# Attention maxima turned by VectorE and written as rows, values taken from the keys' projection, two sequences' mixed weights per step

## The chip, the cores and the metric

The kernel runs on one core of one Trainium2 chip. The time is the device time of one execution in microseconds (us); of several executions the median is given.

## What is computed

Four sequences of 512 tokens, 256 features. A gated network chosen per sequence gives `c`; attention with 16 heads of 16 features, all heads sharing one key and one value, works on `c`; then an expert layer. The change concerns the attention:

```
q = (c @ Wq.T + bq) * 16**-0.5          # 16 heads x 16
k, v = split(c @ Wkv.T + bkv)           # 16 each, shared by the heads
w = softmax(q_rows @ k.T)               # q_rows: 16*512 rows per sequence
x = x + (w @ v, heads side by side) @ Wo.T + bo
x2 = cond2(x, cond_8)                   # weights mixed per sequence from 8 sets
x = x + moe(x2)                         # router, top 2 of 8 experts, gelu
```

All of it is in float32.

## The kernel before

Work is issued in an order written out by hand; each engine (TensorE, VectorE, ScalarE, GpSimd) and SyncE, which issues most DMAs, takes its own instructions strictly in that order and waits on semaphores.

*Layout.* `q` of a sequence is a tile of 128 partitions x 4 x 512. Partition 32j + d, for j from 0 to 3 and d below 16, holds feature d; rows 32j+16 to 32j+31 are zero. `k` has the same four groups of 32 rows (the same keys four times), with ones in rows 32j+16 to 32j+31. So a matmul over 32 rows gives q.k, and a number put into row 32j+16 (`HD` is 16) of the query side is added to the scores. Four such matmuls, on the four groups of 32 rows, run on TensorE side by side.

*Units and steps.* A unit `u` is a quarter of the rows of a sequence (`b, hg = divmod(u, 4)`), 16 in all; a step is a quarter of a unit, 64 in all. The loop at L1049 goes over `n`. In step n it issues

- `maxima(m)` (L379) for m = n + 6: four matmuls L388 into PSUM banks, of which tag "m" has three and tag "x" four, and four VectorE reductions L392 to negated row maxima in `negm`;
- `exponentials(n)` (L412): four matmuls L420 of keys with shifted queries `qs`, and ScalarE's exponential L421;
- `weigh(n - 1)` (L426): eight matmuls L435 that weigh the values with the exponentials; after the fourth step of a unit a copy L444 and a DMA L445 to DRAM (`od`);
- the side work of the step, from the lists `beside` and `last` (L724 to L759): projections of the next sequence, and normalising, output projection, routing of the former ones.

A matmul of float32 is two records in the profile, a transpose one. A *pass* below is two maxima and two exponentials, in four row groups at once. In a *dense* step (side work on TensorE, L1071) the order is pass, side work, pass, all of `weigh`; in an *open* step (L1083) it is pass, half of `weigh`, pass, side work, other half.

*The shift.* `shifted(u)` (L396), at steps with m % 4 == 1, turns `negm` with four TensorE transposes L402 into one bank, so that the maxima lie in rows 32j+16, and VectorE adds that bank to the unit's columns of `q` (L406). The sum `qs` is what `exponentials` reads.

*Side work touched.* `queries` (L316) projects half of the queries, ScalarE brings them to `stage`, and SyncE copies them in eight DMAs L327 into `q`; `q` alternates between two tiles. `keys` L333 and `values` L340: the values are eight matmuls L345 of 32 columns with the tokens as stationary operand, then VectorE adds the bias L349. The values tile has 32 columns, those from 16 on are one, so the same matmul gives the softmax sum. In the steps of sequence b (k = n % 16): queries of b+1 at k = 0 and 1, keys at 2, values at 3. `values` of `finish` (L451), at k = 2, is of another kind: it loads sums (L456) and weighed values (L460) of sequence b-1 back from `od`; `inverse` (L482), at k = 3, takes their reciprocal on VectorE (L485), writes it (L486) and reads it back spread out (L490). Sequence 0 has its projections before the loop, where `hidden` and `down` (the gated network) fill TensorE.

*Mixed weights.* While sequence 0 is in the loop, `turn_mixed` (L690: four transposes L695 and a ScalarE copy) and `route_mixed` (L701: matmuls L707 with the router) prepare one sequence each: steps 5, 7, 9, 11 turn, steps 6, 8, 10, 12 route (`behind`, L762).

After the loop the expert layer streams its weights; TensorE is busy there throughout.

Of the kernel before, what the change touches and what calls it, by code (L numbers as in the profile page):

```python
# [17 lines left out]
P = 128  # L18
B = 4
# [22 lines left out]
def adaln_attn_ffn_kernel(  # L42
# [9 lines left out]
    bk: bass.AP,  # L52
    wv: bass.AP,
    bv: bass.AP,
    wo: bass.AP,
# [132 lines left out]
    bk_sb = load(bk, [P, 1], "bk_sb")  # L188
    wv_sb = load(wv, [P, 2, 32], "wv_sb")
    bv_sb = load(bv[0:1, :].to_broadcast([P, 32]), [P, 32], "bv_sb")  # L190
    wo_sb = load(wo, [P, 2, D], "wo_sb")
# [48 lines left out]
    for n in range(2):  # L240
        t = const.tile([P, 4, 4, 32], F32, name=f"negm{n}")
        nc.gpsimd.memset(t, 0.0)
        negm.append(t)

    q_tiles = []
    for n in range(2):
        t = const.tile([P, 4, T], F32, name=f"q{n}")
        nc.gpsimd.memset(t, 0.0)
        q_tiles.append(t)

    def mixed(b, g):
# [47 lines left out]
    seqs = [{} for _ in range(B)]  # L299
    qs_of = {}  # L300
    e_of = {}
# [9 lines left out]
    def project(b):  # L311
# [4 lines left out]
        def queries(co):  # L316
            def piece():
                pq = bank("x")
                for c in range(2):
                    mm(pq, wq_sb[:, c, ts(co, P)], coT[:, c, ts(b, T)], start=c == 0, stop=c == 1)  # L320
                qd = qp.tile([P, T], F32, name="stage", bufs=4)
                nc.scalar.activation(
                    qd, pq, AF.Identity, bias=bqs_sb[:, co : co + 1], scale=HD**-0.5
                )
                for n in range(2):
                    for j in range(4):
                        nc.sync.dma_start(  # L327
                            s["q"][32 * j : 32 * j + HD, 2 * co + n, :],
                            qd[ds(64 * n + HD * j, HD), :],
                        )  # L330
            return piece

        def keys():  # L333
            s["k"] = qp.tile([P, T], F32, name="k")
            pk = bank("x")
# [4 lines left out]
        def values():  # L340
            s["v"] = qp.tile([P, 4, 32], F32, name="v")
            pv = bank("x")
            for sc in range(4):
                for c in range(2):
                    mm(  # L345
                        pv[:, ts(sc, 32)], coT[:, c, ds(b * T + sc * P, P)], wv_sb[:, c, :],
                        start=c == 0, stop=c == 1,
                    )
            nc.vector.tensor_tensor(  # L349
                s["v"], pv[:, 0:P].rearrange("p (s d) -> p s d", s=4),  # L350
                bv_sb.unsqueeze(1).to_broadcast([P, 4, 32]), ALU.add,
            )
# [26 lines left out]
    def maxima(m, js):  # L379
# [6 lines left out]
        for j in js:  # L386
# [5 lines left out]
            nc.vector.tensor_reduce(  # L392
                nm[:, i, j, HD : HD + 1], pm, AX.X, ALU.max, negate=True
            )

    def shifted(u):  # L396

        b, hg = divmod(u, 4)
        nm = negm[u % 2]
        pt = bank("x")  # L400
        for i in range(4):
            nc.tensor.transpose(  # L402
                pt[:, ts(i, P)], nm[:, i].rearrange("p j d -> p (j d)"), ident
            )
        qs = qp.tile([P, 512], F32, name="qs")
        nc.vector.tensor_tensor(  # L406
            qs.rearrange("p (i t) -> p i t", i=4), pt.rearrange("p (i t) -> p i t", i=4),
            seqs[b]["q"][:, :, ts(hg, P)], ALU.add,
        )
        qs_of[u] = qs  # L410

    def exponentials(n, js):  # L412
# [4 lines left out]
        for n4, j in enumerate(js):  # L417
            px = bank("m" if n4 >= 2 else "x")
            rows_j = slice(32 * j, 32 * j + 32)
            mm(px, k[rows_j, ts(sc, P)], qs_of[u][rows_j, :], start=True, stop=True)  # L420
            nc.scalar.activation(  # L421
# [339 lines left out]

    behind = {5 + 2 * b + n: (f, b) for b in range(B) for n, f in enumerate((turn_mixed, route_mixed))}  # L762

# [10 lines left out]
    def side(b, k):  # L774
# [14 lines left out]
        if b == 0 and k in behind:  # L789
            f, to = behind[k]  # L790
            f(to)


# [8 lines left out]
    for m in range(LEAD):  # L802
        maxima(m, (0, 1, 2, 3))
        if m == 5:
            shifted(0)
# [243 lines left out]
    for n in range(STEPS + 1):  # L1049
# [7 lines left out]
        )  # L1057
        turning = m <= STEPS + 1 and m % 4 == 1
        if m >= STEPS:
            if n < STEPS:  # L1060
                exponentials(n, (0, 1, 2, 3))
            if turning:
                shifted(m // 4 - 1)
            if n == STEPS:
# [6 lines left out]
        elif dense:  # L1071

            maxima(m, (0, 1))
            exponentials(n, (2, 3))
            if turning:
                shifted(m // 4 - 1)
            side(b, k)
# [5 lines left out]
        else:  # L1083
# [6 lines left out]
            exponentials(n, (0, 1))  # L1090
            if turning:
                shifted(m // 4 - 1)
            side(b, k)
            if n > 0:
                weigh(n - 1, (0, 1))

    places = itertools.count()
# [73 lines left out]
def _layouts(i):  # L1171
# [8 lines left out]
    def quarters(w):  # L1180
# [14 lines left out]
    wk = np.zeros((P, 2, 4, 32), f32)  # L1195
    wk[..., :HD] = wkv[:, :, None, :HD]
    bk = np.ones((4, 32), f32)
    bk[:, :HD] = bkv[:HD]
    wv = np.zeros((P, 2, 32), f32)
    wv[..., :HD] = wkv[..., HD:]  # L1200
    bv = np.ones((1, 32), f32)
    bv[0, :HD] = bkv[HD:]
    bias2 = i["L0_cond2_bias"]
# [12 lines left out]
        "bk": bk.reshape(P, 1),  # L1216
        "wv": wv,
        "bv": bv,
        "wo": halves(i["L0_attn_Wo"].T),
# [33 lines left out]
```

## Time and profile before

| | |
|---|---|
| median of 3 runs | 688.33 us (687.2 to 688.59) |
| profiled execution | 676.98 us |
| its span, first to last instruction | 675.3 us |
| granted TensorE clock | 0.994 |
| attention steps, in the span | about 107 to 394 us |

| stretch of the span (us) | TensorE busy | VectorE busy | ScalarE busy |
|---|---|---|---|
| 0 to 75 (gated network) | 72.53 | 30.44 | 14.54 |
| 75 to 107 (its end, first maxima) | 32.00 | 20.70 | 4.81 |
| 107 to 394 (attention steps) | 284.14 | 203.06 | 157.99 |
| 394 to 675 (expert layer) | 267.77 | 75.43 | 48.47 |

| group | line | count | mean ns of one |
|---|---|---|---|
| maxima, matmul records | L388 | 500 | 639 |
| exponentials, matmul records | L420 | 512 | 639 |
| weighing, matmul records | L435 | 1024 | 387 |
| reduction to maxima | L392 | 256 | 685 |
| transposes of the maxima | L402 | 64 | 286 |
| adding them to q | L406 | 16 | 682 |
| values, matmul records | L345 | 64 | 271 |
| their bias | L349 | 4 | 290 |

In profile lines PE is TensorE, DVE VectorE, ACT ScalarE, POOL GpSimd, SP SyncE; "SPq" is what its queue issues. A timeline line has start and duration in us, engine, line, operation, output and inputs, and a count of merged instructions. Matmuls are pipelined, so their durations overlap; distances between starts tell what a group takes.

### The profile page before, as it was taken

To read this page: it belongs to the slowest core of one execution; us is meant where nothing else is said; L and a number is where in the kernel's file an instruction comes from. 1 tells how busy PE (TensorE), PEld (TensorE's weight loads), DVE (VectorE), ACT (ScalarE), POOL (GpSimd) and SP (SyncE) were. 2 spreads that over 40 slices of the span, in tenths; PEclk is the share of its full clock that TensorE was granted. 3 is DMA by queue.
4 is the path that set the end of the run, shared out by engine and by line. 5 is a ranking of instruction groups with operands and counts; after the bars stand their busy time and mean duration, and the time that the engine had idled before them with its cause. 6 is when DMAs were issued, how large, how long until landed. Compare 5 with 4: busy or idle time off the path is not lost.

```text
span 675.3 us, 10833 instructions
## 1 busy us (share of the span) xinstructions
PE 656.4 (97%) x4106; PEld 406.9 (60%) x4106; DVE 329.6 (49%) x782; ACT 225.8 (33%) x400; POOL 118.0 (17%) x149
## 2 busy tenths in 40 slices
PE   8999999999999999999999999999999999999992
PEld 3444433444344433443335368888999999988881
DVE  1174855666667677766897754264222222221110
ACT  1122114555554555455553651222111111121110
POOL 1710000000000000310013041135332222232331
PEclk9999999999999999999999999999999999999997
DMA  6931992100031101330024199537989999975311
GB/s 215 376 108 28 248 259 66 33 17 17 11 96 56 48 17 54 116 103 17 21 85 166 64 323 336 161 106 232 277 255 329 330 323 317 337 235 153 82 22 26
DMA packets 63483, 102.40 MB, mean 152 GB/s; under 512 B 6464, under 2 KB 26560, under 8 KB 63296
## 3 DMA queue, kind: packets, MB, share of 16 engines
q1 hardware_dynamic: 47536, 81.51, 35.7%
q0 software_dynamic: 7008, 10.56, 7.6%
q10 hardware_dynamic: 8880, 9.57, 5.5%
q8 instruction: 34, 0.56, 0.3%
q14 instruction: 25, 0.20, 0.1%
HBM read 75.37 MB, written 24.15 MB: 147 GB/s over the span
## 4 chain that ended last, share of the span: by engine, by line
PE 92%; DVE 3%; DMA 2%; issue 1%; POOL 0%; ACT 0%; SPq 0%; POOLq 0%; DVEq 0%
PE ps_m L983 19%; PE ps_m L388 19%; PE ps_x L1013 17%; PE ps_a L435 9%; PE ps_a L286 4%; PE ps_x L270 4%; PE ps_x L288 4%; PE ps_x L420 3%; PE ps_x L547 2%; PE ps_x L320 2%; PE ps_x L515 2%; PE ps_x L402 1%; DVE negm L392 1%; PE ps_x L337 1%; PE ps_a L968 1%; PE ps_x L345 1%
## 5 line engine op out<-in xcount | busy, mean ns | idle before, releaser
L392 DVE TENSOR_REDUCE negm<-ps_m 128x1 f32<-128x512 f32 x250 | 160.6, 685 | 73.3 <-PE ps_x L420 60.1
L421 ACT ACTIVATE e<-ps_x 128x512 f32<-128x512 f32 x244 | 132.4, 594 | 119.8 <-PE ps_x L420 115.9
L388 PE MATMUL ps_m<-k,q 32*128 32x512 f32 x500 | 150.4, 639 | 0.1
L420 PE MATMUL ps_x<-qs,k 32*128 32x512 f32 x488 | 139.9, 639 | 0.0
L983 PE MATMUL ps_m<-xT,wi_sb 128*128 128x128 f32 (+1 forms) x800 | 130.3, 321 | 0.0
L1013 PE MATMUL ps_x<-wo_sb,e 128*128 128x256 f32 x576 | 128.5, 379 | 0.0
L983 PEld LDWEIGHTS ps_m<-xT,wi_sb 128*128 128x128 f32 x800 | 119.0, 191 | 10.1 <-issue 0.4
L1013 PEld LDWEIGHTS ps_x<-wo_sb,e 128*128 128x128 f32 x576 | 107.6, 190 | 13.7
L987 ACT ACTIVATE e<-ps_m 128x512 f32<-128x512 f32 x72 | 42.8, 597 | 194.1 <-PE ps_m L983 192.6
L1024 POOL DMA_INDIRECT out_dram<-y,to_row x36 | 56.1, 1558 | 140.5 <-DMA out_dram<-y,to_row 74.4
L388 PEld LDWEIGHTS ps_m<-k,q 32*128 32x128 f32 x500 | 44.6, 183 | 54.3 <-issue 23.9
L435 PE MATMUL ps_a<-e,v 128*32 128x256 f32 x1024 | 73.7, 387 | 1.4 <-ACT stage L444 1.0
L435 PEld LDWEIGHTS ps_a<-e,v 128*32 128x32 f32 x1024 | 24.2, 108 | 70.6 <-issue 54.4
L970 DVE COPY xT<-ps_a 128x256 f32<-128x256 f32 (+1 forms) x23 | 12.2, 529 | 95.1 <-PE ps_a L968 95.1
L1023 DVE TENSOR_SCALAR y<-ps_x,w 128x256 f32<-128x256 f32 x36 | 17.4, 482 | 81.2 <-PE ps_x L1013 81.2
L665 POOL DMA_INDIRECT xp<-x,to_i x32 | 33.2, 1038 | 57.7 <-DVE negm L392 34.1
L420 PEld LDWEIGHTS ps_x<-qs,k 32*128 32x128 f32 x488 | 38.6, 183 | 3.3 <-issue 2.6
L597 POOL TENSOR_SCALAR x<-mk 128x4 f32<-128x4 f32 x4 | 0.8, 210 | 219.6 <-DVE mk L594 219.5
L291 DVE SCALAR_TENSOR_TENSOR hid<-ps_x,wo_sb,sg 128x512 f32<-128x512 f32 x16 | 12.0, 749 | 47.1 <-PE ps_x L288 44.1
L286 PE MATMUL ps_a<-xT_sb,wi_sb 128*128 128x512 f32 x64 | 30.5, 598 | 0.9 <-DMA wi_sb<-in_wcond_dram 0.9
L288 PE MATMUL ps_x<-xT_sb,wi_sb 128*128 128x512 f32 x64 | 30.1, 592 | 0.0
L270 PE MATMUL ps_x<-hid,wo_sb 128*128 128x512 f32 x64 | 28.7, 595 | 0.0
(155 smaller groups left out, 472.6 us busy)
## 6 DMA issues: line engine op xcount, KB each, us to landing
wi_sb<-in_wi_dram SPq DMA_DIRECT2D x25, 1024.0 KB, 8.1
wo_sb<-in_wo_dram SPq DMA_DIRECT2D x25, 1024.0 KB, 8.0
xp<-zeros ACTq DMA_DIRECT2D x1, 8580.0 KB
od<-stage SPq DMA_DIRECT2D x15, 256.0 KB, 2.1
wi_sb<-in_wcond_dram SPq DMA_DIRECT2D x12, 256.0 KB, 5.8
xt<-xp SPq DMA_DIRECT2D x11, 260.0 KB, 5.9
xT_sb<-in_xT_dram SPq DMA_DIRECT2D x4, 512.0 KB, 7.7
w_sb<-in_w_dram SPq DMA_DIRECT2D x8, 256.0 KB, 5.2
```

Source lines behind the costliest of these rows:

```text
L270: mm(po, wd[:, hc, ts(dc, P)], hid_of[b][:, hc, :], start=hc == 0, stop=hc == 3)
L286: mm(pu, wu[:, c, :], xT_sb[:, c, ts(b, T)], start=c == 0, stop=c == 1)
L288: mm(pg, wg[:, c, :], xT_sb[:, c, ts(b, T)], start=c == 0, stop=c == 1)
L388: mm(pm, q[32 * j : 32 * j + 32, i, ts(hg, P)], k[32 * j : 32 * j + 32, :], start=True, stop=True,)
L392: nc.vector.tensor_reduce(nm[:, i, j, HD : HD + 1], pm, AX.X, ALU.max, negate=True)
L420: mm(px, k[rows_j, ts(sc, P)], qs_of[u][rows_j, :], start=True, stop=True)
L421: nc.scalar.activation(e_of[n][:, :, j, :].rearrange("p h (i t) -> p i h t", i=4), px.rearrange("p (i h t) -> p i h t", i=4, h=4), AF.Exp,)
L435: i = mm(pa_of[u][32 * hh : 32 * hh + 32, j0 * P : (j0 + nj) * P], seqs[b]["v"][:, sc, :], e[:, hh, j0 : j0 + nj].rearrange("p j n -> p (j ...
L983: mm(ph[:, ts(k, n)], wi_of[u][:, c, ts(f0 + k, P)], xT_of[u][:, c, :], start=c == 0, stop=c == 1,)
L987: nc.scalar.activation(hT_of[u][:, f0 : f0 + each].rearrange("p f t -> p (f t)"), ph, AF.Gelu_apprx_tanh,)
L1013: mm(po[:, 0:D], hT_of[u][:, fc, ts(h, P)], wo_of[u][:, fc, :], start=fc == 0, stop=fc == F // P - 1,)
L1024: i = nc.gpsimd.indirect_dma_start(out=out_rows, out_offset=bass.IndirectOffsetOnAxis(ap=to, axis=0), in_=y, in_offset=None, compute_op=AL ...
```

## The change

- `shifted(u)` no longer uses TensorE. VectorE transposes `negm`, now one column per maximum (128 x 4 x 32), in blocks of 32x32 into a tile `nmT`; then four DMAs from SyncE, one for each 32 tokens, write the maxima straight into the rows 32j+16 of `q`, 4 partitions x 4 x 128 bytes each. `exponentials` reads `q` itself, four pieces of 128 columns that lie 512 apart; `qs` is gone. `shifted` is issued at the end of steps with m % 4 == 3, two steps earlier than before.
- As `q` tiles are used again for sequences 2 and 3, their rows 32j+16 are set back to zero, one DMA ahead of every four query copies.
- The weights of the values are put into spare rows of the keys' weights (rows 32j+17 to 32j+24 for j = 0 and 1, eight features each), which meet zero rows of `q`. `values` is now four TensorE transposes of `k`, and a VectorE copy of 16 columns into one of two tiles that were filled with ones. The matmuls, the bias and the two loads for them are gone.
- `behind` turns two sequences in step 5 and routes them in step 7, the other two in 9 and 11; steps 6, 8, 10 and 12 have no such work, and are open.

```diff
         def values():
-            s["v"] = qp.tile([P, 4, 32], F32, name="v")
+            s["v"] = v_tiles[b % 2]
             pv = bank("x")
             for sc in range(4):
-                for c in range(2):
-                    mm(
-                        pv[:, ts(sc, 32)], coT[:, c, ds(b * T + sc * P, P)], wv_sb[:, c, :],
-                        start=c == 0, stop=c == 1,
-                    )
-            nc.vector.tensor_tensor(
-                s["v"], pv[:, 0:P].rearrange("p (s d) -> p s d", s=4),
-                bv_sb.unsqueeze(1).to_broadcast([P, 4, 32]), ALU.add,
+                nc.tensor.transpose(pv[:, ts(sc, P)], s["k"][:, ts(sc, P)], ident)
+            nc.vector.tensor_copy(
+                s["v"][:, :, 0:HD].rearrange("p s (j d) -> p s j d", j=2),
+                pv.rearrange("p (s j d) -> p s j d", s=4, j=4)[:, :, 0:2, HD + 1 : HD + 9],
             )
...
                 for n in range(2):
+                    if b > 1:
+                        nc.sync.dma_start(s["q"][HD:P:32, 2 * co + n, :], nil[0:4, :])
                     for j in range(4):
...
     def shifted(u):
         b, hg = divmod(u, 4)
-        nm = negm[u % 2]
-        pt = bank("x")
-        for i in range(4):
-            nc.tensor.transpose(
-                pt[:, ts(i, P)], nm[:, i].rearrange("p j d -> p (j d)"), ident
-            )
-        qs = qp.tile([P, 512], F32, name="qs")
-        nc.vector.tensor_tensor(
-            qs.rearrange("p (i t) -> p i t", i=4), pt.rearrange("p (i t) -> p i t", i=4),
-            seqs[b]["q"][:, :, ts(hg, P)], ALU.add,
-        )
-        qs_of[u] = qs
+        nmT = qp.tile([P, 4, 32], F32, name="nmT")
+        nc.vector.transpose(
+            nmT.rearrange("p i t -> p (i t)"), negm[u % 2].rearrange("p i j -> p (i j)")
+        )
+        for a in range(4):
+            nc.sync.dma_start(
+                seqs[b]["q"][HD:P:32, :, ds(hg * P + 32 * a, 32)],
+                nmT[32 * a : 32 * a + 4],
+            )
...
-            mm(px, k[rows_j, ts(sc, P)], qs_of[u][rows_j, :], start=True, stop=True)
+            mm(
+                px, k[rows_j, ts(sc, P)], seqs[u // 4]["q"][rows_j, :, ts(u % 4, P)],
+                start=True, stop=True,
+            )
...
-    behind = {5 + 2 * b + n: (f, b) for b in range(B) for n, f in enumerate((turn_mixed, route_mixed))}
+    behind = {
+        5 + 2 * b + 2 * n: (f, b) for b in range(0, B, 2)
+        for n, f in enumerate((turn_mixed, route_mixed))
+    }
...
             f, to = behind[k]
             f(to)
+            f(to + 1)
...
-        turning = m <= STEPS + 1 and m % 4 == 1
...
-            if turning:
-                shifted(m // 4 - 1)
...
+        if m < STEPS and m % 4 == 3:
+            shifted(m // 4)
...
     wk[..., :HD] = wkv[:, :, None, :HD]
+    wk[:, :, :2, HD + 1 : HD + 9] = wkv[..., HD:].reshape(P, 2, 2, 8)
     bk = np.ones((4, 32), f32)
     bk[:, :HD] = bkv[:HD]
+    bk[:2, HD + 1 : HD + 9] = bkv[HD:].reshape(2, 8)
```

In the prologue `shifted(0)` comes after the fourth set of maxima instead of the sixth.

More of the change, by code (lines that the diff above doesn't have):

```diff
@@ L52, in adaln_attn_ffn_kernel @@
     bk: bass.AP,
-    wv: bass.AP,
-    bv: bass.AP,
     wo: bass.AP,
@@ L188, in adaln_attn_ffn_kernel @@
     bk_sb = load(bk, [P, 1], "bk_sb")
-    wv_sb = load(wv, [P, 2, 32], "wv_sb")
-    bv_sb = load(bv[0:1, :].to_broadcast([P, 32]), [P, 32], "bv_sb")
     wo_sb = load(wo, [P, 2, D], "wo_sb")
@@ L240, in adaln_attn_ffn_kernel @@
     for n in range(2):
-        t = const.tile([P, 4, 4, 32], F32, name=f"negm{n}")
+        t = const.tile([P, 4, 32], F32, name=f"negm{n}")
         nc.gpsimd.memset(t, 0.0)
@@ L249, in adaln_attn_ffn_kernel @@
         q_tiles.append(t)
+    v_tiles = []
+    for n in range(2):
+        t = const.tile([P, 4, 32], F32, name=f"v{n}")
+        nc.gpsimd.memset(t, 1.0)
+        v_tiles.append(t)
     def mixed(b, g):
@@ L299, in adaln_attn_ffn_kernel @@
     seqs = [{} for _ in range(B)]
-    qs_of = {}
     e_of = {}
@@ L392, in maxima @@
             nc.vector.tensor_reduce(
-                nm[:, i, j, HD : HD + 1], pm, AX.X, ALU.max, negate=True
+                nm[:, i, j : j + 1], pm, AX.X, ALU.max, negate=True
             )
@@ L803, in adaln_attn_ffn_kernel @@
         maxima(m, (0, 1, 2, 3))
-        if m == 5:
+        if m == 3:
             shifted(0)
@@ L1074, in adaln_attn_ffn_kernel @@
             exponentials(n, (2, 3))
-            if turning:
-                shifted(m // 4 - 1)
             side(b, k)
@@ L1090, in adaln_attn_ffn_kernel @@
             exponentials(n, (0, 1))
-            if turning:
-                shifted(m // 4 - 1)
             side(b, k)
@@ L1196, in _layouts @@
     wk[..., :HD] = wkv[:, :, None, :HD]
+    wk[:, :, :2, HD + 1 : HD + 9] = wkv[..., HD:].reshape(P, 2, 2, 8)
     bk = np.ones((4, 32), f32)
     bk[:, :HD] = bkv[:HD]
[L1199 to L1202, printed above, removed]
+    bk[:2, HD + 1 : HD + 9] = bkv[HD:].reshape(2, 8)
     bias2 = i["L0_cond2_bias"]
@@ L1216, in _layouts @@
         "bk": bk.reshape(P, 1),
-        "wv": wv,
-        "bv": bv,
         "wo": halves(i["L0_attn_Wo"].T),
```

## The prediction

> **What bounds the kernel now.** I read the page first, then the stretch table, then the timeline around single steps. The page:
>
> ```profile
> PE 656.4 (97%) x4106; PEld 406.9 (60%) x4106; DVE 329.6 (49%) x782; ACT 225.8 (33%) x400; POOL 118.0 (17%) x149
> ```
>
> TensorE is busy 97% of the span; the chain that ended last is 92% TensorE. In the stretch table it is busy 284.14 of the 287 us from 107 to 394 (the attention steps). So TensorE time taken out of attention should come off the end, unless another engine is late next. The groups that the change removes:
>
> ```profile
> L406 DVE TENSOR_TENSOR qs<-ps_x,q 128x512 f32<-128x512 f32 x16 | 10.9, 682 | 0.3 <-PE ps_x L402 0.3
> L402 PE MATMUL ps_x<-ident,negm 128*128 128x128 f32 x64 | 10.5, 286 | 0.0
> L345 PE MATMUL ps_x<-wv_sb,coT 128*128 128x32 f32 x64 | 7.5, 271 | 0.0
> ```
>
> Matmuls overlap, so their price is the distance from their start to the next group's start. The timeline at the third step after a query projection shows it, with the VectorE work that reads the sums:
>
> ```profile
> 193.85 0.66 PE L402 MATMUL ps_x<-ident,negm 128*128 128x128 f32 x4
> ...
> 194.34 1.87 PE L345 MATMUL ps_x<-wv_sb,coT 128*128 128x32 f32 x16
> ...
> 196.14 0.70 PE L388 MATMUL ps_m<-k,q 32*128 32x512 f32 x2
> ...
> 196.46 0.54 DVE L485 RECIPROCAL iv<-sum 128x64 f32<-128x64 f32 x1
> ```
>
> Four transposes take 0.49 us, the values 1.80. In an open step, where a piece of mixing (L435) follows, the same four take 0.58, and the pass after them is stretched:
>
> ```profile
> 327.06 0.66 PE L402 MATMUL ps_x<-ident,negm 128*128 128x128 f32 x4
> 327.64 0.64 PE L435 MATMUL ps_a<-e,v 128*32 128x256 f32 x8
> 328.21 0.70 PE L388 MATMUL ps_m<-k,q 32*128 32x512 f32 x2
> 328.59 0.70 PE L420 MATMUL ps_x<-qs,k 32*128 32x512 f32 x2
> ```
>
> The exponentials' L420 should start with L388, as two of the four row groups; it comes 0.38 later. SyncE's queue just before:
>
> ```profile
> 181.41 4.94 SPq L327 DMA_DIRECT2D q<-stage  x8
> 186.45 0.53 SPq L445 DMA_DIRECT2D od<-stage  x1
> 187.07 5.54 SPq L327 DMA_DIRECT2D q<-stage  x8
> 192.67 0.58 SPq L456 DMA_DIRECT2D sum<-od  x1
> ```
>
> SyncE is full from 181.4 to 194.6: about 0.63 us per issue back to back. The sums' load, issued last, lands 2.1 us later (194.8), 1.7 before L485 wants it. This queue is where the change adds most.
>
> **What the Trainium skill says.** "VectorE: DVE Perf Modes", section "The three transpose paths": VectorE transposes 32x32 blocks only, into SBUF, 311 ns for 128x128 bf16. The trace has no VectorE transpose; I take 0.3 us for f32, between 0.2 and 0.7 (L406 takes 0.68 for four times the columns). "DMA: Bandwidth & Descriptors", section "Anatomy of one DMA", gives a fixed cost of some 2.0 us (fitted there on GpSimd's path); SyncE's q copies here land in 1.9. The same page, "Specifications", says that pieces under 512 B are read, modified and written; the new rows are 128-byte pieces, which no transfer of before shows alone, so I take 2.0 us and up to 4. "Perfetto Trace Analysis", "What "DMA-bound" means": a sequencer solid with DMA issues is itself a bound. The SyncE lines above agree.
>
> **The change, part by part.**
>
> *Maxima turned on VectorE.* Removed: 16 groups of four L402 transposes, 0.49 us in dense steps, 0.58 to 0.59 elsewhere; summed over the block starts, 8.5 us, all on TensorE's path. Also 16 adds L406 of 0.68 on VectorE; after six of the groups in open steps the next pass stretched from 1.07 or 1.33 to 1.43 to 1.76, because the maxima wait for one of three m banks. Added on VectorE: 16 transposes of 0.3. On VectorE the step moves two steps earlier; the reductions behind it wait its 0.3. I take the two together as 0.3 us gained (between -1 and 1.5). Added on SyncE: 64 row copies, four per unit, and 8 zero-row copies for sequences 2 and 3. Added wait: the first exponentials of a unit wait for four landings; behind them on TensorE queue everything else. The exponentials' moving operand is now four pieces of 128 in q. No matmul of before reads with gaps, but L406 reads those same pieces at 682 ns where the gapless maxima take 685, so I put it at nothing.
>
> In an ordinary unit this wait is covered. For steps 29 to 32 the reductions end at about 244.7, transpose at 245.0, the fourth copy starts at 247.0 and lands at 249; the exponentials come at 251.5 (252.13 less the turn). Cover 2.5 us.
>
> *Where SyncE's queue is full.* In the new issue order, the unit's four copies stand behind sixteen q copies plus zero rows and ahead of the sums' load. Steps 16 to 19: from 181.41, nine issues, od, ten issues, four rows: 24 x 0.63 = 15.1, so the sums' load starts at 196.5 and lands at 198.6. VectorE stands at L485 with the reductions of that step behind it. TensorE reaches step 20 at 196.5 (198.21 less 0.49 and 1.25); its second maxima need an m bank, free only after L485 (0.56) and a reduction (0.75): 199.9. Stall 3.4 us; the rows themselves land at 197.9 and are inside it. Steps 32 to 35: from 256.30 the same 24 issues, with od ready late, 271.5; landing 273.6, bank 274.9, wanted 272.5. Stall 2.4. Steps 0 to 3 have no sums and no zero rows: rows land about when wanted, 0.2. If an issue of four partitions costs 0.35 (ivd alone: 0.33), these are 2.1, 1.1 and 0; with the slow issue of 1.14 inside the second eight of the trace, or a later landing, 4.5, 3.5 and 1.
>
> *The last unit.* Its transpose follows the choice of experts in VectorE's order:
>
> ```profile
> 380.15 0.19 DVE L595 TENSOR_TENSOR hot<-rev,mk 128x32 f32<-128x32 f32 x1
> 380.37 0.19 DVE L585 SCALAR_TENSOR_TENSOR left<-hot,pr 128x32 f32<-128x32 f32 x1
> ...
> 381.96 0.69 DVE L406 TENSOR_TENSOR qs<-ps_x,q 128x512 f32<-128x512 f32 x1 [0.27 <-PE ps_x L402]
> ```
>
> It stands between the first two, at 380.35 to 380.65; the fourth copy starts at 382.6 and lands at 384.6. Exponentials of step 60 are wanted at 382.85 (383.44 less 0.59). Stall 1.7 (0.7 to 4).
>
> *Values from the keys.* Sixteen matmul records over 1.80 us become four transposes, 0.55 by L402's spacing: 1.25 x 4 = 5.0 gained. The prologue's one counts: TensorE has no gap there and the q copies, last issued at 67.14, have landed when the maxima come at 70.95. The copy of 128x64 takes no more than L349's 0.29. The transposes need the key activation, one step older: no wait. Two loads of constants fewer, two memsets more, on queues with slack.
>
> *Two sequences per step.* The turned weights and routing columns keep their matmuls. But steps 6, 8, 10 and 12 lose their side work and become open steps: 3.54 us each (319.86 to 323.40 in the timeline: two pieces of mixing at 0.57, passes of 1.33 and 1.07) against 3.14 for a dense step without its side work (two passes of 1.07 and sixteen mixing records in 1.00). That is 1.6 lost, against about 1.0 of stretched passes after L695 saved: -0.6 (between -2 and 0.5).
>
> *Waiting on four semaphores* at each unit's first exponentials: -0.5 (0 to -2), from 51 ns for such an instruction in the L420 view.
>
> **Sum.** 8.5 + 5.0 + 0.3 - 0.6 - 0.5 - (3.4 + 2.4 + 0.2 + 1.7 = 7.7) = 5.0 us saved. Profiled execution: 676.98 us, span 675.3; so 672.0. The median of the runs shown is 688.33, 11.4 above; I take off the same 5.0: **683.3 us**.
>
> **Rivals.**
>
> 1. *The stalls hide or come cheap.* For it: isolated issues take 0.33. Four-partition issues might too, and the wait at L485 then shrinks. Stalls of 3 rather than 7.7, pairing free: 8.5 + 5.0 + 0.3 - 3.5 = 10.3, so 678. Against: back-to-back issues in the trace never go under 0.5.
> 2. *The gain is eaten, no change.* Stalls at the upper end, 4.5 + 3.5 + 1 + 4 = 13: 8.5 + 5.0 + 0.3 - 0.6 - 0.5 - 13 = -0.3, so 688. It needs landings near 4 us.
> 3. *Slower: the exponentials read q with gaps at a price.* A pass of two maxima and two exponentials takes 1.07 for 0.54 per round of four row groups; if the gapped operand slows the exponentials by a tenth, each of the 128 half-steps is 0.11 us longer, 14 us in all: 688.33 - 5.0 + 14 = 697. It decides from 5.0 / 128 = 0.04 us per half-step on. For it: nothing in the trace has such an operand on TensorE. Against: VectorE reads the same pieces at full rate, and ScalarE's permuted L421 takes 594 where a straight copy L444 takes 588.
> 4. *The waits are wider than the code says* (maxima of a later unit waiting for rows of an earlier one). The changed program's waits show none; its price would be in rival 2's size.
>
> **How the numbers follow.** Forecast 0.55, rival 1 0.20, rivals 2 and 4 0.12, rival 3 0.13. About 0.2% (1.4 us) is what a measurement of this kernel can tell from no change. Faster is the forecast with rival 1, 0.75; the same 0.12; slower 0.13. The forecast's own spread, from the ends above, is 679.5 to 687; the range of 676.5 to 689 adds rivals 1 and 2 and leaves rival 3 out.
>
> **What would show it.** Right: no negm transposes on TensorE; the k transposes 0.5 to 0.6 us long; TensorE idle of 2 to 4 us in the step after each of the two later value pieces, with a VectorE reciprocal waiting for the sums' DMA before it; 1 to 2 us idle near the last units' exponentials, put down to the row copies; open steps 6, 8, 10, 12 near 3.5. Wrong: passes of four row groups longer than 1.07 everywhere (rival 3); waits for row copies in ordinary units (landing far above 2 us); or no gap at the reciprocals (rival 1).

## The result, and the profile after

The changed kernel takes 694.17 us (median of 5 runs, 691.73 to 695.44), the kernel before 688.31 beside it: ratio 1.0085, interval 1.0064 to 1.0105. It is slower by 5.9 us where 5.0 less was forecast. The profiled execution took 695.44 us.

The head of its page: busy time by engine, and the clock that TensorE was granted in 40 slices of the span.

```profile
span 693.7 us, 10653 instructions
...
PE 663.0 (96%) x3994; PEld 399.5 (58%) x3994; DVE 323.6 (47%) x782; ACT 226.1 (33%) x400; POOL 116.1 (17%) x151
...
PEclk9999999999999999899998979999999999999997
```

TensorE has 112 instructions fewer and yet is busy 6.6 us longer. The last line says why: the digits 8, 8 and 7 stand where its clock was not full. The same row of before has nines up to the last slice. Work was removed, and some of the rest ran at a lower clock: busy time alone doesn't tell the two apart.

First, what went as the prediction has it. The groups of the turn and of the values (columns: duration in sum, mean ns):

```profile
L403 DVE STREAM_TRANSPOSE nmT<-negm 128x128 f32<-128x128 f32 x16 | 4.9, 307 | 0.4
...
L351 PE MATMUL ps_x<-ident,k 128*128 128x128 f32 x16 | 2.6, 283 | 0.0
...
L352 DVE COPY v<-ps_x 128x64 f32<-128x64 f32 x4 | 0.9, 216 | 0.0
```

The turn on VectorE takes 0.31 us (0.3 was taken). The timeline at the end of step 19 and in step 20 shows the values' transposes, SyncE's queue, and the stall that was forecast there:

```profile
192.30 2.40 SPq L407 DMA_DIRECT2D q<-nmT  x4
192.40 0.66 PE L351 MATMUL ps_x<-ident,k 128*128 128x128 f32 x4
192.99 0.94 PE L391 MATMUL ps_m<-k,q 32*128 32x512 f32 x2
...
194.74 0.56 SPq L459 DMA_DIRECT2D sum<-od  x1
...
196.89 0.55 DVE L488 RECIPROCAL iv<-sum 128x64 f32<-128x64 f32 x1 [2.98 <-DMA sum<-od]
...
198.04 0.69 PE L391 MATMUL ps_m<-k,q 32*128 32x512 f32 x1 [1.62 <-DVE negm L395]
...
200.41 1.22 PE L391 MATMUL ps_m<-k,q 32*128 32x512 f32 x2
200.42 1.22 PE L420 MATMUL ps_x<-q,k 32*128 32x512 f32 x2
201.42 1.06 PE L391 MATMUL ps_m<-k,q 32*128 32x512 f32 x2
```

The transposes take 0.59 from start to start. Four row copies take 2.40 on SyncE, the load of the sums comes after them, VectorE stands 2.98 us for it, TensorE 1.62 for VectorE. All that was predicted, with nearly these sizes. Then comes what was not: the pass at 200.41 runs without any wait, and its records take 1.22 and 1.06 instead of 0.70 and 0.59. The pass takes 2.02 us instead of 1.07. Stretches of the changed kernel with the granted clock (third number from the end) say that it happens in several places:

```profile
120.00:140.00 20.00, 20.00 (x188) 9.46 (x184) 13.64 (x25) 12.27 (x23) 0.00 (x0) 1.00 0.07 21
140.00:145.00 5.00, 5.00 (x40) 1.26 (x36) 1.82 (x4) 1.52 (x3) 0.00 (x0) 0.66 0.00 0
...
200.00:205.00 5.00, 5.00 (x44) 1.50 (x36) 2.08 (x4) 2.62 (x7) 0.00 (x0) 0.74 0.28 90
...
275.00:280.00 5.00, 5.00 (x29) 0.92 (x24) 1.51 (x4) 1.69 (x4) 0.00 (x0) 0.50 0.28 95
365.00:370.00 5.00, 3.44 (x13) 1.93 (x14) 3.54 (x10) 2.31 (x5) 0.00 (x0) 0.64 0.10 32
...
405.00:410.00 5.00, 4.41 (x14) 1.40 (x18) 1.67 (x2) 4.13 (x8) 0.00 (x0) 0.50 1.00 376
```

A clock of 0.50 means half. The record of the clock has half-clock stretches of 3.41 us (three), 6.83 (two) and 10.24 (one) ahead of the last product, 34.1 us together: up to 17 us of TensorE time. The trace of before has none ahead of its last product. That one is of an execution of 676.98 us, though, 11.4 below its median. So there are two questions: what halves the clock, and where the 11.4 us of before lie.

Three theories stood. *Stall and clock*: the waits bring half-clock stretches, and these cost more than the waits. *Parts*: the parts work against each other. *Chip*: the change is worth different amounts on different chips.

### The profile page after: what moved, and what is told of

It reads as the page before. It is cut to its first block, busy times and chain, and to the rows that moved or that the text cites. A ratio compares the mean times of both kernels' runs of the same rounds, so it can differ in the third digit from the quotient of the medians.

```text
span 693.7 us, 10653 instructions
## 1 busy us (share of the span) xinstructions
PE 663.0 (96%) x3994; PEld 399.5 (58%) x3994; DVE 323.6 (47%) x782; ACT 226.1 (33%) x400; POOL 116.1 (17%) x151
## 4 chain that ended last, share of the span: by engine, by line
PE 88%; DMA 4%; DVE 3%; SPq 1%; another core or an unknown queue 1%; issue 1%; POOL 0%; ACT 0%; POOLq 0%; DVEq 0%
PE ps_m L391 19%; PE ps_m L990 18%; PE ps_x L1020 17%; PE ps_a L438 9%; PE ps_a L290 4%; PE ps_x L274 4%; PE ps_x L292 4%; PE ps_x L518 2%; PE ps_x L550 2%; PE ps_x L323 2%; PE ps_x L420 2%; PE ps_x L344 1%; PE ps_a L975 1%; DVE negm L395 1%; SPq L407 1%
## 5 line engine op out<-in xcount | busy, mean ns | idle before, releaser
L391 PE MATMUL ps_m<-k,q 32*128 32x512 f32 x500 | 161.1, 663 | 5.9 <-DVE negm L395 5.9
L420 PE MATMUL ps_x<-q,k 32*128 32x512 f32 x488 | 148.3, 670 | 4.9 <-DVE xT L977 3.3
L990 PE MATMUL ps_m<-xT,wi_sb 128*128 128x128 f32 (+1 forms) x800 | 131.8, 323 | 0.0
L1020 PEld LDWEIGHTS ps_x<-wo_sb,e 128*128 128x128 f32 x576 | 107.6, 190 | 13.7
L391 PEld LDWEIGHTS ps_m<-k,q 32*128 32x128 f32 x500 | 47.6, 189 | 66.5 <-DVE negm L395 33.3
L438 PE MATMUL ps_a<-e,v 128*32 128x256 f32 x1024 | 79.7, 406 | 2.4 <-issue 1.2
L977 DVE COPY xT<-ps_a 128x256 f32<-128x256 f32 (+1 forms) x23 | 12.2, 529 | 99.4 <-PE ps_a L975 94.0
L420 PEld LDWEIGHTS ps_x<-q,k 32*128 32x128 f32 x488 | 40.5, 191 | 8.3 <-DVE xT L977 4.2
L668 POOL DMA_INDIRECT xp<-x,to_i x32 | 31.8, 994 | 59.5 <-DVE to_i L665 28.8
L1028 POOL CAST to_row<-at 128x1 int32<-128x1 f32 x36 | 19.5, 541 | 66.9 <-DVE at L1013 66.8
```

The source lines that it names most:

```text
L391: mm(pm, q[32 * j : 32 * j + 32, i, ts(hg, P)], k[32 * j : 32 * j + 32, :], start=True, stop=True,)
L420: mm(px, k[rows_j, ts(sc, P)], seqs[u // 4]["q"][rows_j, :, ts(u % 4, P)], start=True, stop=True,)
L438: i = mm(pa_of[u][32 * hh : 32 * hh + 32, j0 * P : (j0 + nj) * P], seqs[b]["v"][:, sc, :], e[:, hh, j0 : j0 + nj].rearrange("p j n -> p (j ...
L668: i = nc.gpsimd.indirect_dma_start(out=xp, out_offset=bass.IndirectOffsetOnAxis(ap=to_i[:, k, ch : ch + 1], axis=0), in_=s["x3"][:, ch, 0: ...
L990: mm(ph[:, ts(k, n)], wi_of[u][:, c, ts(f0 + k, P)], xT_of[u][:, c, :], start=c == 0, stop=c == 1,)
L1020: mm(po[:, 0:D], hT_of[u][:, fc, ts(h, P)], wo_of[u][:, fc, :], start=fc == 0, stop=fc == F // P - 1,)
```

## The experiments

### Each part alone

The kernel before, then the pairs of sequences alone, the values alone, and the turn with its rows alone (with before's values, one sequence per step), on one chip.

The values alone are the hunk of `values` with the spare rows of the weights, the turn alone the hunks of `shifted`, `exponentials` and the zero rows. The pairs alone:

```diff
-    behind = {5 + 2 * b + n: (f, b) for b in range(B) for n, f in enumerate((turn_mixed, route_mixed))}
+    behind = {
+        5 + 2 * b + 2 * n: (f, b) for b in range(0, B, 2)
+        for n, f in enumerate((turn_mixed, route_mixed))
+    }
...
             f(to)
+            f(to + 1)
```

> The kernel before, unchanged, to see what its executions look like beside the profiled one (676.98 us, granted clock 0.994), since all of the changed kernel's executions show a granted clock near 0.97. Queue theory (the loss sits in waits behind SyncE's queue): about 688 us, and clocks near 0.994 in every execution, as nothing in the kernel lowers them. Clock theory (TensorE is granted half its clock for some microseconds after stretches in which it idles or does tiny matmuls, and the profiled execution of before happened to be free of that): executions near 688 with a granted clock of 0.975 to 0.985, half-clock stretches in them that the profiled one lacks.

> Only the pairing of two sequences' mixed weights per step, on the kernel before. Queue theory, with the prediction's price: 0.6 us slower, 689, no half clock in steps 7 to 12. Clock theory: the two steps with two routings hold about 2 us of matmuls of 8 columns and are followed by 3.4 us at half clock each, 3 to 4 us slower, 691 to 692, and lines of double length just after L707.

> Only the values from the keys' spare rows, on the kernel before. Both theories: 5.0 us faster (4 times 1.80 less 0.55), 683.3; the queue of SyncE is as before. Clock theory allows another -1 to -4, if the 1.8 us of 32-column matmuls had led to half clock in ordinary executions of before.

> Only the shift: maxima turned on VectorE and written as rows, with the zero rows, the former values and the former one-sequence steps. Queue theory: 8.5 and 0.3 gained, 0.5 and about 6 lost (stalls 1.3 us shorter twice, as the values' matmuls give the queue that time), so 686, 2 us faster. Clock theory: the stalls of 2 to 3 us at steps 20 and 36 and before step 60 are each followed by half clock of 3.4 to 6.8 us, which costs 5 to 10 more: 691 to 696.

Measured (before: 677.45 us on this chip): before again 677.36; pairs 678.29, ratio 1.0017 (1.0010 to 1.0024); values 673.05, ratio 0.9936 (0.9923 to 0.9948); turn 673.86, ratio 0.9949 (0.9936 to 0.9961). The parts give +0.8, -4.4 and -3.6 us, -7.2 in sum: no part alone explains the result. The values' gain and the pairs' loss are near the predicted 5.0 and 0.6. And before itself takes 677 here, not 688.

### The whole, and its waits taken away one by one

The changed kernel; the changed kernel with one sequence per step again (the hunk above undone); with the sums' load on ScalarE's queue:

```diff
-            nc.sync.dma_start(
+            (nc.scalar if b < 2 else nc.sync).dma_start(
                 s["sum"], od[b].rearrange("g (h x) (k n) -> (g h) x k n", h=4, k=8)[:, HD]
             )
```

and a version without the three waits: one sequence per step, the query copies and zero rows of sequences 2 and 3 on GpSimd's queue, the last turn ahead of the choice of experts.

```diff
-                        nc.sync.dma_start(s["q"][HD:P:32, 2 * co + n, :], nil[0:4, :])
+                        nc.gpsimd.dma_start(s["q"][HD:P:32, 2 * co + n, :], nil[0:4, :])
...
-                        nc.sync.dma_start(
+                        (nc.gpsimd if b > 1 else nc.sync).dma_start(
...
             exponentials(n, (0, 1))
+            if m == STEPS - 1:
+                shifted(m // 4)
             side(b, k)
...
-        if m < STEPS and m % 4 == 3:
+        if m < STEPS - 1 and m % 4 == 3:
```

> The changed kernel, unchanged, beside the same kernel before as the single parts were. The parts added up: -4.4 (values) -3.6 (shift) +0.9 (pairing) = -7.1, so a ratio of 0.9895, if nothing joins them. Queue theory: the stalls at steps 20 and 36 are each about 1.2 us longer than with the shift alone, as the values' time is gone: -4.7, ratio 0.993. Clock theory: stalls that are longer by 1.2 us and the two routings in a row bring half-clock stretches that the single parts hardly had (one of 3.4 us in the shift alone): more than the sum by 5 us and more, ratio 0.997 to 1.009.

> The changed kernel with one sequence's mixed weights per step as before. Queue theory: 0.9 us faster than the changed kernel, as the pairing alone cost that. Clock theory: the two half-clock stretches after the paired routings (span 140.8 and 157.8) go as well, 3 to 4 us faster than the changed kernel.

> The changed kernel with the load of the sums of sequences 0 and 1 issued by ScalarE's queue, so that it doesn't stand behind the query copies and rows on SyncE. Queue theory: VectorE's reciprocal at steps 19 and 35 finds its sums; what is left is the wait for the rows, some 1.5 and 0.5 us: 3 us faster than the changed kernel. Clock theory: the half clock after both stalls goes with them if the rest is under about 2 us: 5 to 7 us faster than the changed kernel. If neither stall was what costs: no change.

> A version meant to be faster than both: unpaired, the query copies and zero rows of sequences 2 and 3 on GpSimd's queue, the last unit's transpose ahead of the choice of experts. No stall should be left at steps 20, 36 and 60. Queue theory: 8.5 + 5.0 + 0.3 - 0.5 = 13 us faster than before, ratio 0.981. Clock theory: the same, with a granted clock as before's. If the stalls cost little: ratio 0.99 as the changed kernel's parts.

These runs were on another chip (12), where before takes 686.86. Measured: the changed kernel 690.17, ratio 1.0056 (1.0040 to 1.0072); unpaired 689.72, ratio 1.0034 (1.0018 to 1.0050); sums on ScalarE's queue 686.03, ratio 0.9986 (0.9972 to 0.9999); all three waits gone 680.30, ratio 0.9909 (0.9896 to 0.9922). So the waits at the reciprocals, with what follows them, are worth 4 us, and without any of the waits the change is 6.5 us faster than before even here. Their places were right. Unpairing alone gave 0.5, less than the runs spread. But these runs and those of the parts can't be set side by side: the chip changed with the kernels.

### The same kernels on one chip, and a filled stall

Before, the turn alone, the whole, and the whole with products of zeros where TensorE stands in steps 20 and 36. They add work and take no wait away.

```diff
+            if n in (20, 36):
+                maxima(m, (0,))
+                fill = bank("x")
+                for _ in range(4):
+                    mm(fill, nil[:, 0:P], nil, start=True, stop=True)
+                maxima(m, (1,))
+            else:
                 maxima(m, (0, 1))
             exponentials(n, (2, 3))
```

> The kernel before, unchanged, to get its trace on the chip that the next kernels run on. Its first profile had 676.98 us while its median was 688.3, and another chip gave 677.4 and 686.9. Theory A (the price of an idle TensorE depends on the chip: on one whose median for this kernel is near 687, GpSimd's scatters of rows hold up all engines, and half-clock stretches follow): near 687 us there, with mixing passes of 2.5 to 5 us during the three blocks of scatters at about 288, 360 and 395 us and some 10 us at half clock ahead of 660 us; near 677 with none of it on the other kind of chip. Theory B (the parts of the change work against each other, the chip only shifts everything): the same passes as in the first profile on either chip, and no half clock ahead of the end.

> The turn on VectorE and the rows by SyncE alone (values as before, routings one by one). It gave 3.6 us less than before on a chip at 677. Theory A: on a chip at 687 its stalls at steps 20 and 36 and before the last unit bring half-clock stretches, so +2 to +7 us there; -3.6 again on a chip at 677. Theory B: -3.6 on either chip.

> The changed kernel, whole, on the same chip as the two above. Theory A: +2 to +6 us on a chip at 687, and about the sum of the parts measured singly, -4 to -8 us, on a chip at 677. Theory B: slower than before on either chip.

> The changed kernel, with four products of zeros (512 columns, 0.43 us each, 1.7 us together) put on TensorE between the first and the second matmul of the maxima in steps 20 and 36, where it stands idle for 1.2 to 1.6 us until VectorE's reciprocal is through; no wait is taken away. If the idle stretch is what halves the clock, these two passes stay at 3.9 to 4.4 us, the half-clock stretches after them (3.4 and 6.8 us) go, and the kernel is 2 to 5 us faster than the changed kernel. If the clock falls for another reason, the stretches stay and it is the same or up to 1 us slower.

The chip (6) was of the first kind: before 677.52. Measured: before again 677.20; turn alone 673.00, ratio 0.9940 (0.9926 to 0.9954); the whole **673.95, ratio 0.9949 (0.9934 to 0.9963)**; filled 675.27, ratio 0.9965 (0.9953 to 0.9978). The same changed kernel that loses 5.9 us in the result gains 3.6 here, so the theory of parts can't explain the loss: what the change is worth depends on the chip. The parts do miss their sum, though: singly they gave 7.2 us on a chip of the same kind, together 3.6. The four zero products were too long: they took 3.63 us, 0.91 each, not 0.43, and delayed TensorE, so this kernel is no faster than the changed one; but the half-clock stretches in and after steps 20 and 36 (3.41 us each in the whole) were gone from its trace.

### A shorter fill, a moved scatter, no waits

Two zero products instead of four; the first sequence's scatter of rows ("send", on GpSimd) seven steps later; and the version without waits again.

```diff
         [(1, "v"), (-1, "inv")],
-        [(-2, "send")],
+        [],
...
         [(-1, "mix2"), (-1, "mix3")],
-        [],
+        [(-2, "send")],
```

> The kernel before, once more, to get its trace on a chip where it takes 687 us, should the chip be one. Theory A (the chip decides what the change is worth): if it takes 687, its trace shows passes of 2.5 us or more in the blocks of scatters near 288, 360 and 395 us, where VectorE and ScalarE stand although their operands are there, 7 to 10 us in sum against the trace of 677, and one or two half-clock stretches after them. If it takes 677, none of this. Theory B (the 11 us lie in the weight-bound stages of the experts): passes as at 677, the difference after 400 us.

> The changed kernel, with GpSimd's scatter of the first sequence's rows moved seven steps later (beside step 43 instead of step 36). If the scatter is what holds up VectorE and ScalarE near 290 us on a chip at 687, the hold of 3 to 5 us moves with it, to about 318 us, and none is left at 290; the time stays within 2 us of the changed kernel's. If something else does it at that place (the stall of step 36, the loads of that stretch), the hold stays at 290. On a chip at 677 no hold at either place, and the same time within 1 us.

> The changed kernel with two products of zeros instead of four in the stalled passes of steps 20 and 36. Four took 3.63 us (0.91 each, not 0.43 as I had reckoned), about 2 us more than the idle stretch they were to cover, and took the half-clock stretches away. Two are 1.8 us and fit the idle stretch of 1.2 to 1.6 us. If the idle stretch is what halves the clock: both stretches stay away, and it is 2 to 4 us faster than with four, so 1 to 3 us faster than the changed kernel. If TensorE has to be given as much as four products: one or both stretches are back, and it is within 1 us of the changed kernel.

> The version with none of the three waits (copies of the queries and zero rows of sequences 2 and 3 on GpSimd's queue, the last turn ahead of the routing's choice, routings one by one), which gave 6.5 us less than before on a chip at 687. On a chip at 677: all three stalls (3.1, 2.3 and 1 us) and both half-clock stretches (1.7 us each) of the changed kernel go, so 8 to 10 us less than before; if its gain was one of that chip, 3 to 5 less.

Chip 6 again, before 677.63. Measured: before again 677.22; scatter later 673.94, ratio 0.9947 (0.9931 to 0.9963); two zero products 671.92, ratio 0.9925 (0.9905 to 0.9945); without waits **667.61, ratio 0.9848 (0.9833 to 0.9864)**. The changed kernel at the two stalls on this chip, by stretches:

```profile
193.00:197.00 4.00, 2.42 (x12) 0.78 (x14) 2.77 (x5) 0.14 (x1) 0.00 (x0) 1.00 0.43 122
197.00:201.00 4.00, 4.00 (x28) 1.22 (x24) 1.50 (x3) 2.43 (x5) 0.00 (x0) 0.57 0.23 71
269.50:272.50 3.00, 2.03 (x12) 0.59 (x14) 2.48 (x5) 0.01 (x1) 0.00 (x0) 1.00 0.45 141
272.50:276.00 3.50, 3.50 (x24) 0.80 (x24) 1.00 (x2) 1.50 (x3) 0.00 (x0) 0.51 0.19 50
```

and the same two places with two zero products each:

```profile
192.00:196.00 4.00, 4.00 (x21) 1.28 (x12) 2.13 (x4) 0.59 (x2) 0.00 (x0) 1.00 0.34 98
196.00:200.00 4.00, 4.00 (x42) 1.27 (x40) 2.37 (x5) 2.65 (x5) 0.00 (x0) 1.00 0.21 67
269.00:273.00 4.00, 4.00 (x26) 1.10 (x24) 1.71 (x3) 1.08 (x2) 0.00 (x0) 1.00 0.33 100
273.00:277.00 4.00, 4.00 (x36) 1.48 (x32) 3.75 (x11) 2.65 (x5) 0.69 (x1) 1.00 0.52 181
```

In the first, TensorE is busy 2.42 of 4 us and 2.03 of 3, and the clock falls after it. In the second it is busy throughout with useless work, the stalled pass takes as long (4.03 us against 4.13 at step 20), and the clock stays at 1.00 for both. With useless work the median is 2.0 us lower; the runs overlap (670.45 to 677.03 for the changed kernel, 670.26 to 674.68 with it), so the gain in time isn't clear of noise. The clock is plainer: the mean clock granted to an execution is 0.980 to 0.990 in the changed kernel's 13 runs, 0.989 to 0.992 in the five with four zero products, 0.985 to 0.993 in the six with two. So at these two places the idle stretch, whose waits are 1.58 and 0.97 us in the changed kernel's timeline, brings the half clock, and the price that was missing is that of the clock.

Idle time is not the whole condition, and its length doesn't settle it. In the changed kernel with the moved scatter on chip 6, TensorE waits 1.28 us for the last unit's rows (378.10 to 379.38), and the clock stays full; in one execution of that kernel, 669.62 us, the granted clock is 0.993, as high as before's. In the turn alone, TensorE's idle time at step 20 (1.20 us) brings no half clock on either chip; the only stretch ahead of the last product starts near 268.2, after 3.4 us with no idle time, in the last 1.6 of which TensorE does products of 32 columns. One thing is regular: within each execution the half-clock stretches start whole multiples of 3.413 us apart (the result: 141.15, 158.22, 199.18, 274.27, 366.43, 403.98, so 5, 12, 22, 27 and 11 of them). Where a wait falls between these instants may decide whether it costs; no run tested that.

### The kernel before on a chip where it takes 687

> As the run before it of this kernel, on whatever chip it comes to. On a chip at 687: passes of 2.5 us or more in the blocks of scatters near 288, 360 and 395 us with VectorE and ScalarE standing, 7 to 10 us in sum, and 3 to 10 us more at half clock ahead of 660 us. On a chip at 677: neither.

> As the run before it of this kernel. On a chip at 687: the hold near 290 us moves with the scatter to about 318 us if the scatter causes it, and stays at 290 if not; 690 us within 2. On a chip at 677: no hold at either place, 674 us.

These runs were on a chip (0) of the other kind, before 687.86. Measured: before again 687.83, profiled at 688.29; the moved scatter 697.55, ratio 1.0135 (1.0092 to 1.0178), where 690 was expected. The timeline of the kernel before in the second scatter there:

```profile
361.07 0.70 PE L388 MATMUL ps_m<-k,q 32*128 32x512 f32 x2
361.09 0.70 PE L420 MATMUL ps_x<-qs,k 32*128 32x512 f32 x2
...
362.45 0.42 DVE L520 TENSOR_TENSOR x<-ps_x,x 128x256 f32<-128x256 f32 x1 [2.40 <-PE ps_x L420]
362.85 0.97 POOL L665 DMA_INDIRECT xp<-x,to_i  x1 [0.30 <-issue]
...
363.88 0.42 DVE L520 TENSOR_TENSOR x<-ps_x,x 128x256 f32<-128x256 f32 x1 [1.01 <-remote]
364.59 1.42 DVE L392 TENSOR_REDUCE negm<-ps_m 128x1 f32<-128x512 f32 x2 [0.28 <-PE ps_m L388]
365.34 0.69 PE L388 MATMUL ps_m<-k,q 32*128 32x512 f32 x1 [1.07 <-DVE negm L392]
...
365.36 0.60 ACT L421 ACTIVATE e<-ps_x 128x512 f32<-128x512 f32 x1 [6.90 <-PE ps_m L388]
```

The scores of 361.07 are there by about 361.8, yet VectorE, which has two additions (L520) to do first, reads them at 364.59, and ScalarE at 365.36. But for the first of these additions both stand, one of VectorE's waits put down to nothing in this trace ("remote"), until GpSimd's last issue of the scatter ends at 363.82; VectorE goes on at 363.88, ScalarE 1.5 us later. On chip 6, in the same scatter of the same kernel, they follow their scores (of 358.64) at once:

```profile
359.80 1.29 DVE L392 TENSOR_REDUCE negm<-ps_m 128x1 f32<-128x512 f32 x2 [0.63 <-PE ps_x L420]
...
359.88 1.09 ACT L421 ACTIVATE e<-ps_x 128x512 f32<-128x512 f32 x2 [4.21 <-PE ps_x L420]
```

I call the standing a *hold*. In the third scatter TensorE itself stands without a wait that the trace shows (before, chip 0), and 6.83 us at half clock begin at 399.39, while it stands:

```profile
400.81 2.07 PE L420 MATMUL ps_m<-qs,k 32*128 32x512 f32 x2 [3.81 <-issue]
402.80 1.94 PE L435 MATMUL ps_a<-e,v 128*32 128x256 f32 x16
```

In the kernel with the moved scatter the hold went along with it. Passes between 285 and 293 us take 1.07 us again, and this is the timeline at 319 us:

```profile
319.48 0.70 PE L420 MATMUL ps_x<-q,k 32*128 32x512 f32 x2
...
321.11 1.12 PE L391 MATMUL ps_m<-k,q 32*128 32x512 f32 x2
322.02 0.97 POOL L668 DMA_INDIRECT xp<-x,to_i  x1 [0.31 <-issue]
324.77 1.89 DVE L395 TENSOR_REDUCE negm<-ps_m 128x1 f32<-128x512 f32 x3 [4.40 <-remote]
324.85 1.09 ACT L424 ACTIVATE e<-ps_x 128x512 f32<-128x512 f32 x2 [3.60 <-remote]
325.51 0.69 PE L391 MATMUL ps_m<-k,q 32*128 32x512 f32 x1 [3.28 <-DVE negm L395]
...
328.00 1.22 PE L391 MATMUL ps_m<-k,q 32*128 32x512 f32 x2
```

So the scatters bring the holds on such a chip, by one trace of the moved scatter, and half clock follows this hold too (1.22 at 328.00). On chip 6 the moved scatter changed nothing, and no hold is seen there. The changed kernel with the scatter in its place was not run on chip 0, so what the move itself cost is open.

### The ledger

The starts of the first exponential of steps 6, 14, 18 and so on, from ScalarE's timeline, cut each execution into stretches (us). The first four columns are before and the changed kernel on both kinds of chip, the last the version without waits on chip 6.

| from step, to | what lies there | before, chip 6 | changed, chip 6 | before, chip 0 | changed, result | no waits, chip 6 |
|---|---|---|---|---|---|---|
| start, 6 | | 136.78 | 134.53 | 136.82 | 134.03 | 133.76 |
| 6, 14 | mixed weights | 33.50 | 32.69 | 33.50 | 35.83 | 32.52 |
| 14, 18 | | 18.62 | 17.66 | 18.63 | 17.66 | 17.62 |
| 18, 22 | stall of step 20 | 17.64 | 20.49 | 17.65 | 20.48 | 16.18 |
| 22, 34 | | 57.26 | 54.79 | 57.26 | 54.85 | 55.02 |
| 34, 38 | stall of step 36 | 19.12 | 21.23 | 19.29 | 23.26 | 17.58 |
| 38, 40 | scatter | 11.25 | 10.78 | 13.02 | 13.14 | 10.86 |
| 40, 52 | | 52.87 | 50.13 | 52.87 | 50.13 | 50.29 |
| 52, 56 | scatter | 20.95 | 20.67 | 23.00 | 25.71 | 20.68 |
| 56, 63 | last unit, scatter | 24.27 | 24.81 | 31.13 | 32.46 | 23.92 |
| 63, end | expert layer | 282.83 | 283.28 | 283.42 | 286.18 | 287.88 |
| span | | 675.09 | 671.04 | 686.59 | 693.73 | 666.32 |
| at half clock, ahead of the last 20 us | | 0 | 6.8 | 6.8 | 34.1 | 0 |

Before differs by 11.5 us between the chips, 10.7 of it in the stretches of the scatters. Where there is neither a stall nor a scatter nor paired routing (14 to 18, 22 to 34 and 40 to 52), the change gains the same on both: 6.2 and 6.1 us. The rest differs, and with it the clock. Half of the half-clock time is the most that it can cost: 17.1 - 3.4 = 13.7 us more than before in the result, 3.4 on chip 6. Take that off, and the change saves 6.5 us in the one (7.1 - 13.7) and 7.5 in the other (-4.1 - 3.4). This is a bound, not a measurement: in the stretches of steps 20 and 36 on chip 6, the changed kernel loses 1.47 and 0.69 us against the one with two zero products (19.02 and 20.54), 2.2 of a possible 3.4, so a part of the 13.7 will be longer standing. With that reserve the chip theory and the clock theory are one: on a chip with holds, TensorE idles more, and its clock is halved more often. No run on such a chip takes the half clock away and leaves the waits.

The result's own execution has two further stretches, ahead of steps 8 and 12, just after the paired routings: 20 and 16 records of 8 columns in 2.32 and 1.89 us, no idle time. On chip 12 there was one, on chip 6 none, and unpaired none. That pairing brings them is thus likely, but why they depend on the execution is open. The holds in the result are also longer than before's on chip 0: TensorE stands 2.22 us in the pass at 363 us against 1.07, and in the third scatter VectorE starts nothing for 7.25 us. Whether the changed kernel lengthens them was not tried.

## Why the prediction was wrong, by its own steps

- *"Four transposes, 0.55": 5.0 us for the values.* It is 4.4 measured alone (1.0 to 1.1 us at steps 19 and 35 where 1.25 was taken). Right.
- *The turn on VectorE: 8.5 + 0.3, less 0.5 for the waits, 8.3 net.* At step 63 the version without waits is 13.8 us ahead of before and the values alone 4.3, which leaves 9.5. Right, a little more.
- *Pairs: 0.6 lost.* Alone they lose 0.8 us. Right at 677; where the routings bring half clock, 3.1 more is lost (from step 6 to 14 the changed kernel is 2.3 us behind before in the result and 0.8 ahead on chip 6).
- *Stalls 3.4, 2.4, 1.7.* Against the version without waits, the kernel with two zero products, whose trace has no half clock ahead of the last product, loses 2.84 and 2.96 us in the stretches of steps 20 and 36, and the changed one 1.1 in the last unit (steps 58 to 63: 14.36 against 13.27). The places, the queue and the sizes were right: 6.9 for 7.5. What the prediction put at nothing is what follows a stall: with the clock the two stretches cost 4.31 and 3.65 on chip 6, 4.30 and 5.68 in the result.
- *Rival 3, the gapped queries: slower, 697.* Its number is the nearest to 694.17 and its mechanism is wrong, so that is luck: where the clock is full, records of L420 take 0.70 and 0.59 as before.
- *Rows awaited in ordinary units.* TensorE waits for rows once in the result's trace, 1.29 us in the last unit; in ordinary units never, as forecast, so rival 4 falls too.
- *Rival 1, cheap stalls, and rival 2, "the gain is eaten".* Four row issues back to back take 2.40 us, so the stalls are not cheap. Landings near 4 us are not seen: the last rows, issued at about 389.3, release TensorE at 391.07.
- **The step that failed**: "The median of the runs shown is 688.33, 11.4 above; I take off the same 5.0." Against its own profile the sum was near: 672.0 forecast from 676.98, 673.95 measured (672.75 when profiled) on a chip where before takes 677.5. That is partly luck, as the turn's 1.2 us above its forecast meets 2.2 us of half clock that no term had. The 11.4 us were treated as lying outside the kernel. They lay inside it, in the attention steps: the trace of 677 shows no hold, the trace at 688.29 has three. (The profile at 676.98 probably came from a chip of the first kind: of 57 other runs of before on chips 0 and 12, none is below 685.31. Its chip is not known.) On such a chip TensorE stands idle more and its clock is halved for longer: instead of 5.0 us less, the change took 5.9 more in the result and 3.3 more on chip 12, with 34.1 and 27.3 us at half clock in the traces against 6.8 in before's on chip 0. Without the three waits and the pairing it took 6.5 less on chip 12 and 10.0 less on chip 6. How the loss divides between the half clock and longer holds stays open.

The Trainium skill has this mechanism: "TensorE: Matmul & The Clock Gate", section "Why this matters for your kernels", warns of gaps of more than about 3 us between bursts, and its Part 1 ("What's actually happening") gives a window of some 3.4 us. The traces agree with the window: every stretch ahead of the last product is a multiple of 3.41 us long. They disagree with the gap: 1.58 and 0.97 us of idle time, in passes in which TensorE was busy 2.42 of 4 and 2.03 of 3 us, were enough. The prediction priced the waits at their length.

## What to carry to other kernels

When a profile stands 1.7% below the median of the runs, find where the difference lies before a gain is carried from one to the other; a trace of a run at the median would have shown the holds. Price an idle stretch of TensorE as its length plus a half-clock stretch that may come after it: here stalls of 2.8 and 3.0 us cost 3.7 to 5.7. Where a wait can't be removed, covering it with products that nobody needs can keep the clock full (2.0 us less here at the median, within the spread of the runs). Better is to have no wait: with later query copies on another queue, the last turn earlier and the routings unpaired, the change is 1.5% faster than before on a chip at 677 and 0.9% on one at 687, the best version here on both.

## What was unexpected of the hardware

- Chips differ for the same kernel: 677.5 on two (2 and 6), 686.9 and 687.9 on two others (12 and 0), each within 0.6% over 15 to 35 runs. On the latter, VectorE, ScalarE and at times TensorE stand while GpSimd issues its scatters of rows (VectorE up to 7.25 us in the result, TensorE 3.81 in before on chip 0). What makes a chip one kind or the other is open.
- Half-clock stretches come in multiples of 3.41 us, and their starts in one execution too. They come after idle times as short as 1 to 1.6 us, not after all of these, and at times after 1.6 to 2.3 us of products of 8 or 32 columns with none.
- An isolated issue on SyncE takes 0.32 us, one of four in a row 0.60, however small it is: the 2 KB row copies take as long as the 32 KB query copies.
- In the version without waits, 12.8 us gained up to the last scatter-add's issue become 8.8 of the span: from there to the end it takes 16.3 us on chip 6 and 16.4 on chip 12, in every other kernel traced here 12.2 to 12.9. Unpairing alone doesn't bring it (12.4); which of the other two edits does, the copies on GpSimd's queue or the earlier turn, was not tried.
